# AdaLN-conditioned FFN on one Trainium2 core: another order of the first matmul's products, and of what is queued around them

## The chip, the cores and the metric

The kernel runs on one core of a Trainium2 chip. The metric is the device time of one execution in microseconds (us). It was measured three times before the change: median 1011.42 us, from 1010.62 to 1012.57.

The engines are called as in the profile: PE is TensorE, PEld its weight loads, DVE is VectorE, ACT is ScalarE, POOL is GpSimd and SP is SyncE, which issues DMAs only. All data are float32.

## The reference, cut to what matters

```python
# x: (64 batches, 64 heads, 1024 positions)
K   = 2 * real(einsum('hn,hnl->hl', Cs, exp(dtA[:, :, None] * arange(1024))))   # state-space kernel
y   = irfft(rfft(x * mask) * rfft(K)) + x * mask * D        # causal convolution along the positions
y   = y * mask                                              # "cond": 4096 tokens of width 1024
s   = y @ Wr.T                                              # router, 64 experts of rank 16
G   = zeros.at[top16(s)].set(softmax(top16 values))         # gates
h   = einsum('nd,krd->nkr', y, A)                           # first FFN matmul: 1024 -> 64*16 = 1024
out = x + 2 * einsum('nkr,kdr->nd', h * G[:, :, None], B)   # second FFN matmul: 1024 -> 1024
```

## The kernel before, in words

**Stages.** The 64 heads are eight groups of eight (`g` = 0 to 7), 512 tokens each. For every group the convolution (`conv`) makes `y`, `gates` makes the router's gates, `spread_gates` sends them through DRAM so that each arrives beside the 16 rows that it multiplies (`gx`), and `first` computes the first FFN matmul, multiplies it by the gates into the tile `hg`, and stores `hg` to DRAM. When all groups are done, `second` runs the second FFN matmul, 28 blocks of seven products, from about 668 us to the end. The groups overlap: while the convolution of group g+1 is written down, generators hand out the products of group g piece by piece (`ahead(products, n)`).

**The first matmul** is done by a Strassen-Winograd scheme in `seven`: seven products of half-size factors in place of eight, for each of two halves of the rows (`j` = 0 and 2). One product is 16 matmuls of 128x256. In groups 1 to 7 (`LOW_FROM`) the products 7 and 4 are themselves split in seven (`low`): seven small products of 8 matmuls of 128x128 each, computed for j = 0 and 2 at once and handed out in two parts. Here they are called 7a (its products 1, 6, 7, 2) and 7b (5, 4, 3), likewise 4a and 4b. Between the products DVE combines the results:

- c11 = product 1, to which product 2 is added later in the same PSUM bank; ACT copies the bank to `p1` in between (line 783, shown as `h_p`).
- `u2 = p1 - product 6` (line 793), `u3 = product 7 + u2`, shown as `h_u`.
- c12 = product 5, to which product 3 is added later in the same bank. In between DVE reads the bank to make `c22 = -u3 - c12` (line 829, which calls the helper on line 504; `h_p`), so product 3 waits for c22.
- `u2 = c12 + u2` (line 1193).

So the order of one half is, in groups 1 to 7, 1, 6, 7a, 2, 7b, 5, 3, 4a for j = 0 and 1, 4b, 6, 2, 5, 3 for j = 2.

**Gates.** `finish` allots `hg` and makes the gated quarters: b22, b12 and b21 by POOL (line 1177), b11 by DVE out of the PSUM bank (line 1184). All four are made after product 3 (b21 of j = 0 after 4b). `sums` then makes three sums on DVE (t1 = b11 - b12, b12 = b22 - b12, t2 = b22 + t1) and `last_sum` a fourth, b21 - t2, written over b11. They are run one or two pieces into the next half (`sum_factors`). POOL issues the stores to DRAM (line 1180): b11 and b22 together, b21, then b12, t1, t2, then the fourth sum. There is one buffer of `hg`: the next half's first gate waits until the last store of the one before has landed. The buffers `u2`, `u3` and `p` (for p1 and c22) are two each, and four PSUM banks (`ps_f`) hold all products.

**Order of the queues.** A planner orders each engine's instructions at build time, by the order in which they are written down and by when it takes each to be ready. The trace shows its order, which can differ from the written one. `keep_in_program_order` puts an instruction behind the one written just before it on its engine, `issue_after` behind a named one. On the chip every engine runs its queue in order, so an instruction that waits holds all behind it.

**Left factors.** For the split products 7 and 4, `left_factors` makes sums of weights by DMAs that accumulate, issued by POOL (line 690): twelve of them during group 0, six of which wait for an earlier one to land, and two more in group 1. The first of them to be needed is in product 7a of group 1, at 153.8 us.

Of the kernel before, what the change touches and what calls it, by code (L numbers as in the profile page):

```python
# [107 lines left out]
def body(ctx: ExitStack, tc, x, xo, lens, par, dvec, dgrp, at, bm, wt, cst, out):  # L108
# [601 lines left out]
    def low(n, rights, name, early, late):  # L710
# [22 lines left out]
        q6 = product(6)  # L733
        tt(v2, v2, q6[:, :, :H2], ALU.subtract)
        early(v2)
        q7 = product(7)
        tt(v3, q7[:, :, :H2], v2, ALU.add)
        product(2, c11)
        late((0, 0), c11[:, :, :H2], None, None)
        yield  # L740
        c12 = product(5, more=True)
        late((1, 1), c12[:, :, :H2], v3, v2)
# [6 lines left out]
    def seven(fac, rf, name, finish, second_early, lows):  # L749
# [26 lines left out]
            else:  # L776
                stt(o, v, -1.0, ALU.mult, bank, ALU.subtract)

        u3_of, fourth_of, open_ = {}, [], []
        for j in (0, 2):  # L780
            c11 = product(j, 1, more=True)
            p1 = new(j, "p", 1)
            marks["p1"] = nc.scalar.copy(p1, c11)
            yield j
            for step_ in open_:
                yield j
            early_ = second_early and not j
            if early_:
                product(j, 2, c11)
                yield j  # L790
            p6 = product(j, 6)
            u2 = new(j, "u2")
            marks["u"] = V.tensor_tensor(out=u2, in0=p1, in1=p6, op=ALU.subtract)
            if j in u3_of:
                u3 = u3_of[j]
                tt(u3, u3, u2, ALU.add)
            yield j
            steps_ = iter(())
            if lows and not j:
                u3 = new(j, "u3")  # L800
                other = u3_of[2] = new(2, "u3")

                def early(v, o=u3, u2=u2):
                    tt(o[:, :, hi_], u2[:, :, hi_], v, ALU.add)

                def late(place, bank, v, _, o=u3, u2=u2, other=other):
                    if place[0]:
                        other_half(place, bank, v, other[:, :, (lo_, hi_)[place[1]]])
                    elif place[1]:
                        marks["u"] = V.tensor_tensor(out=o[:, :, hi_], in0=o[:, :, hi_], in1=bank, op=ALU.add)  # L810
                    else:
                        tt(o[:, :, lo_], bank, u2[:, :, lo_], ALU.add)

                steps_ = low(7, low_rights(rf[6], f"{name}_r7"), name, early, late)
                next(steps_)
                yield j
            if not early_:
                product(j, 2, c11)
                yield j
            for _ in steps_:  # L820
                yield j
            if not lows:
                p7 = product(j, 7)
                u3 = new(j, "u3")
                marks["u"] = V.tensor_tensor(out=u3, in0=p7, in1=u2, op=ALU.add)
                yield j
            c12 = product(j, 5, more=True)
            c22 = new(j, "p", 5)
            stt(c22, u3, -1.0, ALU.mult, c12, ALU.subtract)
            if lows and j:  # L830
                for half, v in zip((lo_, hi_), fourth_of):
                    tt(u3[:, :, half], v, u3[:, :, half], ALU.subtract)
            yield j
            if not lows:
                p4 = product(j, 4)
                tt(u3, p4, u3, ALU.subtract)
                yield j
            elif not j:
                rights = low_rights(rf[3], f"{name}_r4")
            product(j, 3, c12)  # L840
            done = finish(j, c11, u2, c12, c22)
            if not lows or j:
                done(u3)
                yield j
                continue
            yield j
            fourth_of[:] = rights[6], rights[0]

            def early(v, o=u3):
                tt(o[:, :, hi_], o[:, :, hi_], v, ALU.subtract)  # L850

            def late(place, bank, v, room, o=u3):
                if place[0]:
                    other_half(place, bank, v, room)
                else:
                    half = (lo_, hi_)[place[1]]
                    tt(o[:, :, half], bank, o[:, :, half], ALU.subtract)

            def rest(steps_, done, u3):
                for _ in steps_:  # L860
                    done(u3)
                    yield

            steps_ = low(4, rights, name, early, late)
            next(steps_)
            open_ = rest(steps_, done, u3)
            yield j


    begun = {}  # L870
# [291 lines left out]
    def first(g, y, spread):  # L1162
# [4 lines left out]
        if g:  # L1167
            rf[:] = right_factors(v, f"ty{g}_")

        def finish(j, c11, u2, c12, c22):  # L1170
            hg = hp.tile([P, 6, 2, HT], F32, tag="hg", name=f"hg_{g}_{j}")

            def gate(m, s):
                return spread[m, j][:, :, s * HT : (s + 1) * HT]

            def gt_(o, a, b, op):
                G.tensor_tensor(out=o, in0=a, in1=b, op=op)  # L1177

            def store(a, b, slot):
                nc.gpsimd.dma_start(hg_dram[g, :, slot : slot + b - a, j : j + 2, :], hg[:, a:b])  # L1180

            b11, b22, b21, b12, t1, t2 = (hg[:, n] for n in range(6))
            def first_quarter():
                i = V.tensor_tensor(out=b11, in0=c11, in1=gate(0, 0), op=ALU.mult)
                if late_gates:
                    tc.keep_in_program_order(i)


            late_gates = g in (0, NG - 1)
            if not late_gates:  # L1190
                first_quarter()
            gt_(b22, c22, gate(1, 1), ALU.mult)
            marks["u"] = V.tensor_tensor(out=u2, in0=c12, in1=u2, op=ALU.add)
            gt_(b12, u2, gate(0, 1), ALU.mult)
            if late_gates:
                first_quarter()
            store(0, 2, 0)

            def sums():
                tt(t1, b11, b12, ALU.subtract)  # L1200
                tt(b12, b22, b12, ALU.subtract)
                tt(t2, b22, t1, ALU.add)
                store(3, 6, 3)

            def last_sum():
                tt(b11, b21, t2, ALU.subtract)
                store(0, 1, 6)

            def done(u3):
                gt_(b21, u3, gate(1, 0), ALU.mult)  # L1210
                store(2, 3, 2)
                unsummed.extend((sums, last_sum))

            return done

        last = None
        for j in seven(wa, rf, f"h{g}", finish, g == 0, g >= LOW_FROM):
            n = 0 if j != last else n + 1
            last = j
            if n in (1, 3 if j and g >= LOW_FROM else 2):  # L1220
                sum_factors(1)
            yield
            if n == 1 and len(rf) == 2:
# [260 lines left out]
    def ahead(it, n):  # L1484
        for _ in range(n):
            next(it, None)
# [17 lines left out]
    for g in range(NG):  # L1504
# [16 lines left out]
            products, done = counted(first(g, y, spread)), [0]  # L1521
        if g + 1 == NG:
            break
        if g == 0:
            made_left = [left_factors(n) for n in (7, 4)]
            for steps_ in made_left:
                ahead(steps_, 3)
        ahead(products, (1, 3)[g] if g < 2 else 2)
        spread_gates(g, ex, spread)
        if g == 0:  # L1530
            tables1, n = steps_of(1), 0
            while True:
# [138 lines left out]
```

## Time and profile before

| | |
|---|---|
| median of the timed runs | 1011.42 us |
| the profiled execution | 1011.2 us, of which its span is 1009.4 and 1.8 lie around it |
| busy: PE, DVE, POOL, ACT | 944.7, 778.2, 372.8, 169.6 us |
| granted TensorE clock, mean | 0.98 |
| first matmul, a product of 16 matmuls | 3.45 us start to start, of 8 small ones 0.89 us |
| `second`, 668 us to the end | PE busy 337.3 of 341.4 us |

The page has a line of engine totals, a strip of 40 slices, the chain of work that ended last, and groups of instructions by line. In a group "x16 | 38.9, 2432" is the count, the busy time in us and the mean of one in ns. The list of waits has, for each pair, the time in us, the number of waits and the longest. In a timeline the first number is the start in us, the second the duration, and a bracket at the end is the idle time just before, with what ended it. In a table of windows the columns are the window, its length, busy time (and instructions) of PE, PEld, DVE, ACT and POOL, the granted clock, the DMA share and GB/s.

### The profile page before, as it was taken

The numbers are of one execution on the slowest core, as the hardware profiler recorded it, in microseconds if no ns is written. First come the engines' busy times: TensorE is split into PE (matmuls) and PEld (weight loads), VectorE is DVE, ScalarE is ACT, GpSimd is POOL, SyncE is SP. The second block draws the span as 40 slices with busy tenths as digits, with TensorE's granted clock in tenths as the row PEclk, the third lists the DMA queues.
The fourth block names the chain that finished last, engine by engine and source line by source line (L and its number), as shares of the span: only waits on it lengthen the run. The fifth ranks groups of instructions, "written<-read, shape, count | busy, mean of one in ns | idle before, by whom it ended". The sixth has DMA issues, their size and how long they took to land.

```text
span 1009.4 us, 15219 instructions
## 1 busy us (share of the span) xinstructions
PE 944.7 (94%) x5720; PEld 759.4 (75%) x5720; DVE 778.2 (77%) x1872; ACT 169.6 (17%) x328; POOL 372.8 (37%) x330
## 2 busy tenths in 40 slices
PE   7997899998998998998998998989999999999998
PEld 2674658677667767857856877878888888888887
DVE  8984889698796796797688459879975785686674
ACT  5351122421311321231130000000000000000000
POOL 0234212132124105115106113236664774554565
PEclk9999899998999998999999999999999999999999
DMA  7769146225433434245235045384475368267432
GB/s 271 203 141 198 57 123 169 99 79 172 137 94 127 149 87 157 84 144 166 85 94 172 33 171 210 104 303 156 155 238 193 104 210 281 84 213 254 128 124 105
DMA packets 74959, 153.21 MB, mean 152 GB/s; under 512 B 10790, under 2 KB 22790, under 8 KB 74886
## 3 DMA queue, kind: packets, MB, share of 16 engines
q1 hardware_dynamic: 52546, 99.65, 30.7%
q0 software_dynamic: 19520, 50.89, 16.4%
q10 hardware_dynamic: 2820, 1.70, 0.6%
q8 instruction: 45, 0.74, 0.3%
q14 instruction: 28, 0.23, 0.1%
HBM read 100.13 MB, written 47.33 MB: 146 GB/s over the span
## 4 chain that ended last, share of the span: by engine, by line
PE 56%; DVE 24%; POOL 5%; issue 2%; DMA 2%; ACT 1%; DVEq 0%; POOLq 0%
PE s L1424 33%; PE h L760 10%; PE h L721 6%; DVE s L927 5%; POOL hg L1177 3%; DVE hg L493 2%; PE pc L992 2%; PE pc L969 2%; PE pu L883 1%; DVE s_more L927 1%; DVE h_u L493 1%; POOL gx L1148 1%; DMA gt_dram<-gt 1%; PE psh L1088 1%; DVE y L1003 1%
## 5 line engine op out<-in xcount | busy, mean ns | idle before, releaser
L760 PE MATMUL h<-y,waa 128*128 128x256 f32 x512 | 119.9, 385 | 0.0
L927 DVE SCALAR_TENSOR_TENSOR s<-s,turn 128x64 f32<-128x64 f32 (+1 forms) x432 | 116.5, 314 | 2.0 <-ACT s L888 1.3
L760 PE MATMUL h<-ty,was 128*128 128x256 f32 x512 | 117.7, 380 | 0.0
L760 PEld LDWEIGHTS h<-y,waa 128*128 128x128 f32 x512 | 97.9, 195 | 13.9 <-issue 0.7
L760 PEld LDWEIGHTS h<-ty,was 128*128 128x128 f32 x512 | 95.5, 190 | 14.8 <-issue 2.7
L1177 POOL TENSOR_TENSOR hg<-h_p,gx 128x512 f32<-128x512 f32 x16 | 38.9, 2432 | 174.3 <-DVE h_p L504 170.5
L1177 POOL TENSOR_TENSOR hg<-h_u,gx 128x512 f32<-128x512 f32 x32 | 45.4, 1419 | 124.3 <-DVE h_u L493 96.1
L760 PE MATMUL h<-y,was 128*128 128x256 f32 x288 | 68.4, 391 | 8.0 <-DVE h_p L504 8.0
L1180 POOL DMA_DIRECT2D hg_dram<-hg x64 | 43.6, 681 | 87.3 <-DVE hg L493 31.3
L760 PEld LDWEIGHTS h<-y,was 128*128 128x128 f32 x288 | 54.4, 194 | 19.4 <-DVE h_p L504 11.1
L1438 ACT COPY p<-s 128x512 f32<-128x512 f32 x28 | 16.4, 586 | 307.9 <-PE s L1424 307.9
L493 DVE TENSOR_TENSOR hg<-hg 128x512 f32<-128x512 f32 x64 | 42.6, 682 | 33.0 <-POOL hg L1177 27.7
L1283 POOL TENSOR_TENSOR o<-o,acc_a 128x512 f32<-128x512 f32 x32 | 47.6, 1508 | 41.3 <-ACT acc_a L1301 10.8
L883 PE MATMUL pu<-x,bt 128*64 128x448 f32 x256 | 53.4, 549 | 3.1 <-DVE y L1003 3.1
L1003 DVE TENSOR_TENSOR y<-pc,mask 128x512 f32<-128x512 f32 x64 | 40.6, 682 | 16.5 <-PE pc L992 16.5
L1148 POOL DMA_DIRECT2D gx<-gt_dram x56 | 34.3, 649 | 50.0 <-DMA gt_dram<-gt 47.2
L1283 POOL TENSOR_TENSOR o<-o,b_room 128x512 f32<-128x512 f32 x32 | 49.6, 1572 | 8.6 <-DVE b_room L493 8.6
L493 DVE TENSOR_TENSOR o<-o,s 128x512 f32<-128x512 f32 x50 | 34.0, 680 | 21.9 <-PE s L1424 16.8
L992 PE MATMUL pc<-s,w 64*64 64x192 f32 (+1 forms) x768 | 42.4, 368 | 7.9 <-DVE s L927 7.9
L1283 POOL TENSOR_TENSOR o<-o,u 128x512 f32<-128x512 f32 x36 | 45.8, 1295 | 10.0 <-DVE u L493 9.7
L721 PE MATMUL h<-h_r,low 128*128 128x128 f32 x224 | 30.4, 279 | 16.3 <-DVE h_r L493 16.3
L883 PEld LDWEIGHTS pu<-x,bt 128*64 128x64 f32 x256 | 17.4, 137 | 35.7 <-issue 16.7
(313 smaller groups left out, 1941.8 us busy)
## 6 DMA issues: line engine op xcount, KB each, us to landing
x<-in_x SPq DMA_DIRECT2D x32, 512.0 KB
o<-in_xo SPq DMA_DIRECT2D x64, 256.0 KB
out<-o SPq DMA_DIRECT2D x63, 256.0 KB
gx<-gt_dram POOLq DMA_DIRECT2D x56, 256.0 KB, 4.5
qy<-hg_dram SPq DMA_DIRECT2D x28, 512.0 KB
r<-hg_dram SPq DMA_DIRECT2D x26, 512.0 KB
hg_dram<-hg POOLq DMA_DIRECT2D x16, 768.0 KB, 5.2
hg_dram<-hg POOLq DMA_DIRECT2D x16, 512.0 KB, 4.7
```

The lines of the kernel that those rows point to most:

```text
L493: V.tensor_tensor(out=o, in0=a, in1=b, op=o_)
L721: nc.tensor.matmul(bank[:, ii, :H2], lhsT=LOW[n][i - 1][:, k, ii * P : (ii + 1) * P], rhs=rights[i - 1][:, k, :], start=(first and ii == 0 ...
L760: nc.tensor.matmul(bank[:, ii, :], lhsT=fac[n - 1][:, k, (j + ii) * P : (j + ii + 1) * P], rhs=rf[n - 1][:, k, :], start=(first and ii == ...
L883: nc.tensor.matmul(pu[hh * NS : (hh + 1) * NS, :], lhsT=bt[:, i, (1 - c) * P + hh * NS : (1 - c) * P + (hh + 1) * NS], rhs=xt[:, hh, : NCH ...
L927: return V.scalar_tensor_tensor(out=o, in0=a, scalar=scalar, in1=b, op0=op0, op1=op1)
L992: m = nc.tensor.matmul(pcs[hh][half_of(e, late), into], lhsT=w[o : o + NS, c, i, seg : seg + HP], rhs=s[o : o + NS, c, of].rearrange("p k ...
L1003: marks["y"] = V.tensor_tensor(out=y[:, :, i // 2, 2 * (i % 2) + hh, :], in0=pcs[hh].rearrange("p (k b) -> p k b", b=NB), in1=mask, op=ALU ...
L1148: i = queue.dma_start(gx[:, ii, :], gt_dram[g, c * n : (c + 1) * n, :].unsqueeze(1).to_broadcast([n, RANK, TOK]),)
L1177: G.tensor_tensor(out=o, in0=a, in1=b, op=op)
L1180: nc.gpsimd.dma_start(hg_dram[g, :, slot : slot + b - a, j : j + 2, :], hg[:, a:b])
L1283: tc.keep_in_program_order(G.tensor_tensor(out=o, in0=a, in1=b, op=op_))
L1424: nc.tensor.matmul(bank[:, ii, :], lhsT=left_[i - 1][:, k, ii * P : (ii + 1) * P], rhs=right_[i - 1][:, k, :], start=(first and ii == rows ...
```

## The change

In groups 1 to 7 the order of the products becomes 1, 5, 6, 7a, 3, 7b, 2, 4a for j = 0 and 1, 5, 4b, 6, 3, 2 for j = 2: again fourteen pieces, handed out at the same places of the convolution. Product 5's bank is copied to `p5` by ACT, and c22 is made later out of `p5`, in place. Products 1 and 5 thus both hold their banks until products 2 and 3 are added. The four gated quarters are made as their inputs come: b12 after product 3, b22 after u3 is whole, b11 after product 2, b21 after 4b (for j = 2, b12, b22 and b21 after product 3, b11 after product 2). `sums` and `last_sum` are run two pieces apart, after the third and the fifth piece of a half's successor instead of the second and the third (fourth for j = 2); `last_sum` writes over t1 instead of b11. Within a split product, product 2 comes ahead of product 7. Group 0 keeps its order of products, but makes b21 ahead of b12. In the main loop the left factors' DMAs are written behind the gates' DMAs of group 0 instead of ahead of them.

```diff
@@ low
         early(v2)
+        product(2, c11)
+        late((0, 0), c11[:, :, :H2], None, None)
         q7 = product(7)
         tt(v3, q7[:, :, :H2], v2, ALU.add)
-        product(2, c11)
-        late((0, 0), c11[:, :, :H2], None, None)
         yield
@@ seven, groups 1 to 7 (group 0 keeps the old order in a branch of its own)
+        def first_two(j):
+            c11 = product(j, 1, more=True)
+            p1 = new(j, "p", 1)
+            marks["p1"] = nc.scalar.copy(p1, c11)
+            yield c11, p1
+            c12 = product(j, 5, more=True)
+            p5 = new(j, "p", 5)
+            nc.scalar.copy(p5, c12)
+            yield c12, p5
...
+        def into_22(p5, u3):
+            marks["u"] = V.scalar_tensor_tensor(
+                out=p5, in0=u3, scalar=-1.0, in1=p5, op0=ALU.mult, op1=ALU.subtract)
+            return p5
...
+        seventh = low(7, low_rights(rf[6], f"{name}_r7"), name, early, late)
+        next(seventh)
+        yield 0
+        product(0, 3, c12)
+        last_12(c12, u2)
+        yield 0
+        next(seventh)
+        last_22(into_22(p5, u3))
+        yield 0
+        product(0, 2, c11)
+        last_11(c11)
+        rights = low_rights(rf[3], f"{name}_r4")
+        yield 0
...
+        fourth = low(4, rights, name, early, late)
+        next(fourth)
+        yield 0
+        steps = first_two(2)
...
+        next(fourth)
+        last_21(u3)
+        yield 2
+        u2 = sixth(2, p1)
+        tt(other, other, u2, ALU.add)
+        yield 2
+        last_12, last_22, last_11, last_21 = finish(2)
+        product(2, 3, c12)
+        last_12(c12, u2)
+        last_22(into_22(p5, other))
+        for half, v in zip(halves, (rights[6], rights[0])):
+            tt(other[:, :, half], v, other[:, :, half], ALU.subtract)
+        last_21(other)
+        yield 2
+        product(2, 2, c11)
+        last_11(c11)
+        yield 2
@@ finish
+            def last_12(c12, u2):
+                marks["u"] = V.tensor_tensor(out=u2, in0=c12, in1=u2, op=ALU.add)
+                gt_(b12, u2, gate(0, 1), ALU.mult)
+            def last_22(c22):
+                gt_(b22, c22, gate(1, 1), ALU.mult)
+            def last_21(u3):
+                gt_(b21, u3, gate(1, 0), ALU.mult)
+                store(2, 3, 2)
+                unsummed.append(last_sum)
+            def last_11(c11):
                 i = V.tensor_tensor(out=b11, in0=c11, in1=gate(0, 0), op=ALU.mult)
                 if late_gates:
                     tc.keep_in_program_order(i)
+                store(0, 2, 0)
+                unsummed.insert(0, sums)
...
             def last_sum():
-                tt(b11, b21, t2, ALU.subtract)
-                store(0, 1, 6)
+                tt(t1, b21, t2, ALU.subtract)
+                store(4, 5, 6)
@@ first
-            if n in (1, 3 if j and g >= LOW_FROM else 2):
+            if n in ((1, 2) if g < LOW_FROM else ((2, 4) if j == 0 else (2, 4))):
                 sum_factors(1)
@@ the main loop
+        ahead(products, (1, 3)[g] if g < 2 else 2)
+        spread_gates(g, ex, spread)
         if g == 0:
             made_left = [left_factors(n) for n in (7, 4)]
             for steps_ in made_left:
                 ahead(steps_, 3)
-        ahead(products, (1, 3)[g] if g < 2 else 2)
-        spread_gates(g, ex, spread)
```

## The prediction

> **What bounds the kernel now.** I read the engine totals first, then the waits of PE and DVE, then the timelines around the longest of them, then a table by stage.
>
> ```profile
> PE 944.7 (94%) x5720; PEld 759.4 (75%) x5720; DVE 778.2 (77%) x1872; ACT 169.6 (17%) x328; POOL 372.8 (37%) x330
> ```
>
> PE's products fill the span, so only time in which PE stands still, or runs at a lower clock, is to be had: 1009.4 - 944.7 = 64.7 us, and the low clock. The second matmul has next to none of it (341.4 us, 337.3 busy) and the change does not touch it. The waits of PE, and under them the two of DVE that are not for PE, say whom it waits for in the rest:
>
> ```profile
> PE h L721 <- DVE h_r L493: 16.3, 6, 3.1
> PE h L760 <- DVE h_p L504: 8.0, 7, 2.9
> PE pc L992 <- DVE s L927: 7.9, 2, 7.5
> PE h L721 <- DVE ty L504: 4.6, 4, 1.3
> PE h L721 <- DVE h_u L793: 4.6, 6, 1.0
> ```
>
> ```profile
> DVE hg L493 <- POOL hg L1177: 27.7, 10, 4.5
> DVE hg L1184 <- DMA gx<-gt_dram: 15.2, 1, 15.2
> ```
>
> PE waits for DVE, and DVE itself waits for POOL's gates and for one late transfer. The same stretch comes once a group; here it is in group 5, from the timeline:
>
> ```profile
> 460.70 4.60 POOL L1177 TENSOR_TENSOR hg<-h_p,gx 128x512 f32<-128x512 f32 x1
> ...
> 466.62 1.28 POOL L1177 TENSOR_TENSOR hg<-h_u,gx 128x512 f32<-128x512 f32 x1
> ...
> 469.46 1.28 POOL L1177 TENSOR_TENSOR hg<-h_u,gx 128x512 f32<-128x512 f32 x1
> ...
> 470.77 0.69 DVE L493 TENSOR_TENSOR hg<-hg 128x512 f32<-128x512 f32 x1 [4.39 <-POOL hg L1177]
> ...
> 473.48 1.13 PE L721 MATMUL h<-h_r,low 128*128 128x128 f32 x8 [3.12 <-DVE h_r L493]
> ...
> 475.52 3.56 PE L721 MATMUL h<-y,was 128*128 128x128 f32 x16 [0.91 <-DVE h_u L793]
> ```
>
> DVE reaches `sums` of the previous half and stands 4.39 us for the third gate, b12, which ends at 470.74. The factors of product 7a (`h_r`) and u2 lie behind it in DVE's queue, so PE stands 3.12 and 0.91 us. In group 0 the late transfer does the same (timelines of POOL, DVE and PE):
>
> ```profile
> 80.28 0.85 POOL L690 DMA_DIRECT2D low<-low  x1 [3.79 <-DMA low<-low]
> 80.87 3.90 POOL L1148 DMA_DIRECT2D gx<-gt_dram  x6
> ...
> 89.04 0.69 DVE L1184 TENSOR_TENSOR hg<-h,gx 128x512 f32<-128x512 f32 x1 [15.22 <-DMA gx<-gt_dram]
> ...
> 100.25 0.92 PE L992 MATMUL pc<-s,w 64*64 64x192 f32 x8 [7.49 <-DVE s L927]
> ```
>
> ACT sends the gates to DRAM at 64.87, but POOL is busy with the left factors until 80.87, so b11's factor comes at 89.0. DVE then does the recurrences (L927) 15 us late, and PE runs dry. Each such dry spell is followed by a low clock (the granted clock is the last number but two):
>
> ```profile
> 84.00:137.00 53.00, 40.09 (x295) 29.80 (x296) 39.31 (x110) 6.19 (x15) 17.33 (x20) 0.84 0.61 155
> 380.00:460.00 80.00, 73.13 (x516) 56.98 (x514) 64.50 (x187) 19.31 (x35) 20.68 (x22) 0.96 0.39 124
> 460.00:538.00 78.00, 72.34 (x517) 56.60 (x517) 61.07 (x176) 13.42 (x25) 21.21 (x23) 0.98 0.37 118
> ```
>
> **Group 0: the transfers in their new order.** The gates' data can go when they are in DRAM: 64.87 + 3.1 (group 5: sent at 455.80, first `gx` issued at 458.88) = 68.0. An issue takes 0.62, so the first pair is out by 69.3 and lands 4.5 later by the median of its line (3.5 to 11.2): 73.7, from 72.7 to 80.4. DVE arrives at b11 at 73.8. It waits 0 to 6.7 instead of 15.2; I take 2, so DVE runs 13 us ahead. Its unbroken work from 89.65 to the end of c22 at 120.35 (30.7 us) then ends near 107. PE reaches that product at 92.76 + 3.03 + 3 x 3.45 = 106.1. So of PE's idle time between 84 and 137 (7.49, 0.39, 2.87 and 2.16 for the convolution's results, 12.9 in all) about 11 goes; 1.0 of the last stays, as in later groups (1.03), and 0.6 before c22. The low clock costs 53 x 0.16 = 8.5 us of half-filled time, 5.5 of it while PE works; I take 4 back. Gain 15. The ceiling is 12.9 + 5.5 = 18. What moves: twelve DMA issues of the left factors, 31 us of POOL's queue from 50.05 to 81.1, now start near 73 and would end at 104 or later. First use is at 153.8, so that hides. But the gates of group 0 (92.3 to 97.2) share that queue. If all stood behind it, they would end near 109, and `sums`, at 102.02 now, would be 7 us late: the low end is -7. I expect them between the DMAs: these leave POOL idle 3.0 to 3.8 us six times, and the planner does mix the two (in group 1 two left-factor DMAs, at 123.91 and 124.86, run ahead of a gate, at 126.56, that is written before them).
>
> **Groups 2 to 6: the sums two products on.** Between product 3 of j = 2 and `sums` lie now two products (1 and 6, 6.9 us); after the change four (2, 1, 5, 6; 13.8 us). POOL needs 3 x 1.3 us for the three gates, or 4.6 + 2 x 1.3 with the slow one, from about 1 us after product 3: done by 5 to 9 us, so DVE finds them ready. The stalls in front of 7a are gone: 2.77 + 4 x 3.12 for `h_r` and 1.04 + 0.91 + 0.64 + 0.91 + 0.91 for u2, 19.7 us. The low clock of the stages of groups 2 to 6 (82 x 0.04, 80 x 0.02, 80 x 0.04, 78 x 0.02, 70 x 0.02) is 11.1 us, about 10 while PE works; all of it lies just behind 7a, so 10 goes with the stall. The row that decides this is a dry spell of 3.12 us, which sufficed for a low clock.
>
> The Trainium skill (TensorE: Matmul & The Clock Gate, Part 1) says that the clock halves after an idle window of about 3.4 us. By that, spells of 3.12 would cost nothing and these 10 us would not come back; the trace shows the low clock behind each, and I go by it.
>
> **ACT's copy of the fifth product.** Fourteen copies more at 0.586 us (line 783) are 8.2 us on an engine that is busy 17%; they hide beside product 6, and product 3 comes more than 7 us later. PE no longer waits for c22: 0.89, 0.94, 0.93, 0.94, 0.93 and 0.50 in groups 1 to 6, 5.1 us. c22 stays one DVE instruction of 0.68. A copy needs a free `p`, so it waits for POOL's b22 of the half before: ready 10.5 us after that half's product 3, the gate done by 9. If POOL is 1 us late or more, ACT holds the copy inside 7a too, but 4 us of cover lie there. I take nothing.
>
> GPSIMD Engine Reference (of the skill) warns that its data path is shared with DVE instructions of two SBUF inputs, and c22 becomes one. The slow gate, 4.60 us beside DVE's wide sums, agrees, and in price it would be some 0.7 us of POOL per half.
>
> **Two banks held through 7a and 4b.** Products 1 and 5 hold two of the four banks, so small product 6 needs the bank that u2 frees. After the small product before it (0.89) u2 needs a pick-up of about 0.25 (product ends seen in the timeline) and 0.68: 0.04 us late if DVE is free, more by what runs there (0.2 to 1.7). I take 0.6 there, 0.3 for small product 7 and 0.3 in 4b: 1.2 x 7 groups = 8 us, between 0 and 20. The waits for `ty` (4.6 us, 4b behind the router's DVE work) get a product of cover more; I take nothing for that, at most 4.6.
>
> **The sum.** 15 + 19.7 + 10 + 5.1 - 8 = 41.8. From the profiled execution's 1011.2 (0.2 below the median) that is 969.4; I say 969. Group 7 is filled by DVE (54.28 of 60 us), so I expect no more there.
>
> **Rivals.** (1) DVE's stall comes back in another place, or the planner runs `sums` where it likes: `sums` of j = 0 ran at 506.60, ahead of 4b (521.7), though written behind it. Then 7a and its clock stay: 969 + 19.7 + 10 = 999, or 991 if the banks then cost nothing. For it: DVE's order is the planner's, and POOL's 4.6 us was not foreseen. Against: twice the distance. (2) Slower: `last_sum` now overwrites t1, which is still being read by the store of 768 KB that `sums` sets off; before it overwrote b11, whose store left 8 us earlier (465.85 to 473.93). Price: issue 0.7 and landing 5.2 after the sums' 2.0 us, 7.9, against two products of cover (6.9) and about 1 us of other DVE work: nothing at the median, but at the longest landing (8.8) 3.6 us in each of 14 halves, in front of u2, plus a wait for the single `hg` buffer, since the next half's gates are written just ahead of `last_sum`: one more store of 256 KB, 0.7 + 3.9 on POOL and, through b11, on DVE. If the second alone reaches PE, 14 x 4.6 = 64 us: 969 + 64 = 1033. It makes the kernel slower from 41.8 / 14 = 3.0 us a half. Against: DVE waited for these stores twice, 5.2 us in all. (3) The move has no effect, because the left factors' transfers still go first: 969 + 15 = 984.
>
> **Numbers.** Forecast with its bank costs 0.60 (955 to 984), rival 1 0.18, rival 3 0.05, rival 2 0.17. Best case 1011.2 - 18 - 34.8 - 4.6 = 954. From 954 to 1005 leaves out about 0.2. A time within 0.2% (2 us, what a measurement here can tell) of before needs rival 2 at just its turning point: 0.03. Faster 0.80, slower 0.17.
>
> **What would show it.** Right: `gx` of group 0 issued near 68, DVE's wait in front of b11 under 7 us, no 7.5 us gap of PE near 93; no wait of DVE `hg` for POOL above 1 us; PE's waits for `h_r` under 3 us in all, `h_p` near none, waits for u2 in L721 of 0.3 to 1 us, more often than now; granted clock 1.00 in groups 2 to 6. Wrong: DVE `hg` or L1184 waiting for a store (`hg_dram`) for several us a half, or PE's waits for `h_u` above 20 us.

## The result: slower, and the profile after

The changed kernel takes 1043.33 us (median of 4 runs, 1040.55 to 1044.71) against 1011.33 before: a ratio of 1.0312 (95% interval 1.0287 to 1.0336). The forecast was 969. The profiled execution took 1044.08 us with a span of 1042.3; lines behind the diff stand 40 later than before (u2 of product 6: L829; u2 of `last_12`: L1226; POOL's gates: L1217).

The engine totals, with share of the span and instruction count:

```profile
PE 951.0 (91%) x5720; PEld 765.2 (73%) x5720; DVE 800.2 (77%) x1872; ACT 178.6 (17%) x342; POOL 357.2 (34%) x330
```

Of the 32.9 us by which the span grew, PE stands still for 26.6 more (1042.3 - 951.0 = 91.3 against 64.7) and is busy 6.3 longer at the same instruction count, which goes with the lower granted clock (mean 0.961 against 0.980). Neither half of the forecast's gain came; both moved the other way.

The waits of PE, then those of DVE (total us, times, longest):

```profile
PE h L721 <- DVE h_u L829: 37.5, 7, 7.9
PE h L721 <- DVE h_u L504: 10.0, 4, 3.5
PE pu L923 <- DVE y L1043: 8.4, 1, 8.4
PE s L1464 <- DVE acc_a L493: 7.9, 1, 7.9
PE h L721 <- ACT y L732: 7.1, 1, 7.1
...
PE h L760 <- DVE h_p L504: 2.8, 1, 2.8
```

```profile
DVE hg L493 <- DMA hg_dram<-hg: 41.5, 8, 9.9
...
DVE hg L493 <- POOL hg L1217: 3.0, 2, 1.6
```

What was to go did go: no row names `h_r`, `h_p` fell from 8.0 to 2.8, and DVE's waits for POOL's gates from 27.7 to 3.0. In their place PE waits 37.5 us for u2 of product 6, seven times, and DVE 41.5 us for stores to `hg_dram`. (The wait called "in front of 7a" stands, before and after, just behind 7a's first small product.) These are the two signs that the forecast named as showing it wrong. Group 5's timeline (POOL, then DVE, then PE) shows how they hang together:

```profile
478.20 2.13 POOL L1217 TENSOR_TENSOR hg<-h_u,gx 128x512 f32<-128x512 f32 x1
...
485.51 1.81 POOL L1188 DMA_DIRECT2D gx<-gt_dram  x3
487.28 0.80 POOL L1220 DMA_DIRECT2D hg_dram<-hg  x1
...
482.04 1.28 DVE L967 SCALAR_TENSOR_TENSOR s<-s,turn 128x64 f32<-128x64 f32 x1
483.25 1.28 DVE L493 TENSOR_TENSOR hg<-hg 128x512 f32<-128x512 f32 x2
...
489.69 0.27 DVE L967 SCALAR_TENSOR_TENSOR s_more<-s_more,turn 128x64 f32<-128x64 f32 x1
495.25 0.69 DVE L493 TENSOR_TENSOR hg<-hg 128x512 f32<-128x512 f32 x1 [5.29 <-DMA hg_dram<-hg]
495.86 0.68 DVE L829 TENSOR_TENSOR h_u<-h_p,h 128x512 f32<-128x512 f32 x1
...
487.65 1.05 PE L721 MATMUL h<-y,was 128*128 128x128 f32 x8
496.60 1.65 PE L721 MATMUL h<-h_r,low 128*128 128x128 f32 x6 [7.89 <-DVE h_u L829]
```

The sums end near 484.5. Their store of 768 KB goes out only at 487.28, behind three `gx` issues on POOL, and lands near 495.2. DVE runs recurrences (L967) until 489.9 and then stands 5.29 us with the fourth sum, which must not overwrite t1 before the store has read it. u2 could run when product 6 ends at about 487.7, but stands behind both, although it is written two pieces ahead of the fourth sum. The next small product needs the bank that u2 frees, so PE stands 7.89 us.

Group 0, by the timelines of POOL, DVE and PE:

```profile
67.50 4.85 POOL L1188 DMA_DIRECT2D gx<-gt_dram  x8 [17.53 <-DMA gt_dram<-gt]
...
73.57 0.68 DVE L1238 TENSOR_TENSOR hg<-h,gx 128x512 f32<-128x512 f32 x1
...
109.02 5.41 PE L760 MATMUL h<-y,was 128*128 128x256 f32 x16 [2.83 <-DVE h_p L504]
...
118.80 1.78 POOL L690 DMA_DIRECT2D waa<-waa  x1
119.83 1.55 POOL L1220 DMA_DIRECT2D hg_dram<-hg  x1
...
130.53 0.69 DVE L493 TENSOR_TENSOR hg<-hg 128x512 f32<-128x512 f32 x1 [9.94 <-DMA hg_dram<-hg]
...
131.88 2.51 PE L923 MATMUL pu<-x,bt 128*64 128x448 f32 x6 [8.36 <-DVE y L1043]
```

The product behind c22, before the change:

```profile
120.41 5.34 PE L760 MATMUL h<-y,was 128*128 128x256 f32 x16 [2.87 <-DVE h_p L504]
```

The transfers start where the forecast put them (67.50; b11 at 73.57 without a wait), and that product starts at 109.02 instead of 120.41. Then the store of the sums goes out behind the last of the left factors' transfers, the fourth sum waits 9.94 us, and PE stands 8.36. The same happens at the other end of the kernel: the last half's fourth sum runs inside the second matmul, which the forecast took as untouched, waits 9.61 us for its store, and PE stands 7.9 us for DVE's `acc_a` behind it.

The granted clock by stretches (the last number but two) fell just where it was to rise. These are group 2 before, then groups 2 and 5 after (group 5 before, 0.98, stands in the prediction):

```profile
218.00:300.00 82.00, 74.52 (x521) 58.29 (x522) 70.07 (x208) 19.32 (x35) 24.03 (x26) 0.96 0.42 124
...
222.00:304.00 82.00, 66.28 (x470) 50.66 (x469) 64.36 (x187) 24.18 (x42) 13.49 (x18) 0.88 0.43 123
470.00:556.00 86.00, 75.38 (x520) 59.29 (x519) 64.50 (x177) 14.57 (x27) 19.63 (x23) 0.92 0.33 106
```

### The profile page after: what moved, and what is told of

It is laid out like the page before. It is cut to its first block, busy times and chain, and to the rows that moved or that the text cites. A ratio compares the mean times of both kernels' runs of the same rounds, so it can differ in the third digit from the quotient of the medians.

```text
span 1042.3 us, 15267 instructions
## 1 busy us (share of the span) xinstructions
PE 951.0 (91%) x5720; PEld 765.2 (73%) x5720; DVE 800.2 (77%) x1872; ACT 178.6 (17%) x342; POOL 357.2 (34%) x330
## 4 chain that ended last, share of the span: by engine, by line
PE 51%; DVE 22%; DMA 7%; issue 5%; POOL 3%; ACT 2%; DVEq 0%; POOLq 0%; ACTq 0%
PE s L1464 30%; PE h L760 7%; PE h L721 6%; DMA hg_dram<-hg 6%; DVE s L967 4%; PE pc L1032 2%; POOL hg L1217 2%; DVE ty L493 2%; PE pu L923 1%; DVE hg L493 1%; DVE y L1043 1%; PE pc L1009 1%; DVE h_u L493 1%; PE psh L1128 1%; DMA rmag<-rows_of 1%
## 5 line engine op out<-in xcount | busy, mean ns | idle before, releaser
L967 DVE SCALAR_TENSOR_TENSOR s<-s,turn 128x64 f32<-128x64 f32 (+1 forms) x432 | 127.6, 341 | 2.6 <-ACT s L928 2.2
L1217 POOL TENSOR_TENSOR hg<-h_u,gx 128x512 f32<-128x512 f32 x32 | 48.7, 1538 | 216.6 <-DVE den L498 95.3
L493 DVE TENSOR_TENSOR hg<-hg 128x512 f32<-128x512 f32 x64 | 45.2, 722 | 45.2 <-DMA hg_dram<-hg 41.5
L760 PE MATMUL h<-y,was 128*128 128x256 f32 x288 | 70.9, 392 | 2.8 <-DVE h_p L504 2.8
L721 PE MATMUL h<-h_r,low 128*128 128x128 f32 x224 | 35.5, 308 | 37.5 <-DVE h_u L829 37.5
L721 PEld LDWEIGHTS h<-h_r,low 128*128 128x128 f32 x224 | 31.9, 216 | 41.8 <-DVE h_u L829 39.4
L1323 POOL TENSOR_TENSOR o<-o,acc_a 128x512 f32<-128x512 f32 x32 | 47.6, 1506 | 41.4 <-DMA qy<-hg_dram 10.8
L493 DVE TENSOR_TENSOR o<-o,s 128x512 f32<-128x512 f32 x50 | 34.0, 681 | 23.0 <-PE s L1464 17.9
L967 DVE SCALAR_TENSOR_TENSOR s_more<-s_more,turn 128x128 f32<-128x128 f32 x144 | 47.1, 327 | 0.0
```

What stands on the lines that cost most here:

```text
L493: V.tensor_tensor(out=o, in0=a, in1=b, op=o_)
L721: nc.tensor.matmul(bank[:, ii, :H2], lhsT=LOW[n][i - 1][:, k, ii * P : (ii + 1) * P], rhs=rights[i - 1][:, k, :], start=(first and ii == 0 ...
L760: nc.tensor.matmul(bank[:, ii, :], lhsT=fac[n - 1][:, k, (j + ii) * P : (j + ii + 1) * P], rhs=rf[n - 1][:, k, :], start=(first and ii == ...
L967: return V.scalar_tensor_tensor(out=o, in0=a, scalar=scalar, in1=b, op0=op0, op1=op1)
L1323: tc.keep_in_program_order(G.tensor_tensor(out=o, in0=a, in1=b, op=op_))
```

## The experiments

Two theories stood at the start. The theory of the store: the fourth sum's wait is the loss. The theory of the banks: u2 is wanted at once in 7a, and anything ahead of it on DVE is the loss. Each time below is a median; each ratio is to the kernel before in the same runs, whose medians lay between 1010.44 and 1013.73.

### Parts of the change, undone or done alone

**The fourth sum back over b11**, in the changed kernel:

```diff
-                tt(t1, b21, t2, ALU.subtract)
-                store(4, 5, 6)
+                tt(b11, b21, t2, ALU.subtract)
+                store(0, 1, 6)
```

> The changed kernel with one line put back: the fourth sum is written over b11 again instead of t1. Theory of the store (the fourth sum waits for the store that the three sums before it have just set off, and u2 and the evictions queue behind it on DVE): DVE's waits for stores of hg fall from 41.5 us to under 8, and with them PE's gaps that are their image, 20 us in front of product 7a in groups 2 to 6, 8.4 in group 0 and 7.9 at the start of the second matmul; about 36 us less: 1000 to 1012 us. Theory of the banks (products 1 and 5 hold two of four banks, so small product 6 waits for u2 whatever DVE does just before): the waits for stores go too, but PE's wait for u2 at L829 stays above 25 us of its 37.5, and the time stays above 1022.

1032.33 us, ratio 1.0208 (1.0182 to 1.0233); the time and PE's wait are as the theory of the banks had them. The line is worth 11 us of the 32. The waits of DVE and of PE:

```profile
DVE hg L493 <- DMA hg_dram<-hg: 19.1, 7, 7.5
...
PE h L721 <- DVE h_u L829: 31.9, 7, 6.8
```

DVE's wait more than halves, PE's in front of 7a hardly moves: b11 has a store of its own to wait for, and recurrences fill the rest.

**The same line alone in the kernel before** (that diff read backwards):

> The kernel before with the one line changed: the fourth sum is written over t1, nothing else. Theory of the store: the fourth sum follows the three within 1 to 3 us there, and the store takes 0.7 us to issue and 5.2 to land, so DVE waits 3 to 6 us in most of the sixteen halves and PE behind it: 1030 to 1060 us. Theory of the banks: order and banks are those of before, so 1008 to 1015 us.

1024.77 us, ratio 1.0139 (1.0124 to 1.0154), between the two expectations: the line costs 14 us in the old order too.

**The left factors' transfers behind the first gates, alone in the kernel before:**

```diff
+        ahead(products, (1, 3)[g] if g < 2 else 2)
+        spread_gates(g, ex, spread)
         if g == 0:
             made_left = [left_factors(n) for n in (7, 4)]
 ...
-        ahead(products, (1, 3)[g] if g < 2 else 2)
-        spread_gates(g, ex, spread)
```

> The kernel before with only the left factors' transfers written behind the gates of group 0. As forecast: DVE's 15.2 us wait in front of b11 in group 0 goes, PE's 7.5 us gap near 100 us too, and the kernel gains 10 to 18 us: 993 to 1001. Rival: the later left factors delay the gates and stores of group 0 on POOL and in the DMA queue, DVE waits there instead, and the time stays within 5 us of 1011.

1003.58 us, ratio 0.9933 (0.9916 to 0.9950): a gain of 7, between the two expectations. DVE's timeline says where the rest stayed:

```profile
120.30 2.02 DVE L493 TENSOR_TENSOR hg<-hg 128x512 f32<-128x512 f32 x3 [8.19 <-POOL hg L1177]
```

The sums wait 8.19 us for the last gate, which stands on POOL among the transfers, and PE 9.41 us later on for `y`.

**That part undone in the changed kernel** (the same lines read backwards):

> The changed kernel with the left factors' transfers written ahead of the gates again. If that move alone gains 10 to 15 us, as forecast, this is slower than the changed kernel's 1043: 1052 to 1060. Rival: in the changed kernel the last left factors' transfers run just ahead of the stores that the fourth sum of group 0 waits 9.9 us for, and moving them back takes that wait away and gives the gain of the move back elsewhere: 1040 to 1048.

1057.57 us, ratio 1.0479 (1.0437 to 1.0521): 14 us slower, so inside the change the move gained about what was forecast.

### What stands ahead of u2

Four runs of the changed kernel with DVE's queue reordered in front of 7a. **Recurrences of pairs 2 and 3 behind u2:**

```diff
-            marks["u"] = V.tensor_tensor(out=u2, in0=p1, in1=p6, op=ALU.subtract)
+            marks["u"] = marks["six"] = V.tensor_tensor(out=u2, in0=p1, in1=p6, op=ALU.subtract)
 ...
-        recur(2, 3)
+        with tc.issue_after(marks["six" if g > 1 else "u"].ins):
+            recur(2, 3)
```

> After the change, with the recurrences of pairs 2 and 3 queued on DVE behind u2 of product 6 of j = 2 (groups 2 to 6) instead of wherever the planner puts them. In group 5 u2 stood ready at 487.65 and ran at 495.86: until 489.9 behind recurrences, then behind the fourth sum, which waits for the 768 KB store that lands at 495.2. Theory of the store: the landing alone sets the time, taking the recurrences away leaves the DVE waits for the store larger by what they covered (41.5 to about 55 us) and PE's wait in front of 7a near 37 us: 1040 to 1045. Theory of the queue (whatever stands ahead of u2 while small product 6 lacks a bank costs PE its length): the recurrences cost about 3.5 us a half in groups 2 to 6, so PE's wait falls to 20 us or less: 1022 to 1030.

1040.20 us, ratio 1.0265 (1.0230 to 1.0300), as the theory of the store had it. (In the trace the recurrences follow u2 of j = 0, at 494.64 in group 5, and not of j = 2, as the expectation says.) DVE's wait for stores grew from 41.5 to 66.0 us and PE's for u2 fell only to 31.2: the recurrences had run inside the wait and cost little while it lasted.

**The fourth sum behind the u2 written last** (that of product 3, L1226):

```diff
-                tt(t1, b21, t2, ALU.subtract)
+                with tc.issue_after(marks["u"].ins):
+                    tt(t1, b21, t2, ALU.subtract)
```

> After the change, with the fourth sum (still into t1, still behind the 768 KB store) queued on DVE behind the u2 sums of the small products and of the next half, so that its wait stands ahead of nothing that PE needs at once. Theory of the store: PE's wait in front of 7a falls from 37.5 us to the part that the recurrences make (about 16 us): 1018 to 1025, clearly better than the fourth sum over b11 (1032). Theory of the queue: the place is taken by the recurrences and by the gates written behind it, PE's wait in front of 7a stays at 25 to 32 us as with the sum over b11: 1028 to 1036.

1023.70 us (1016.24 to 1027.10), ratio 1.0096 (1.0066 to 1.0126). It gains 20, more than the 11 of writing over b11; what remains in front of 7a (26.8 us in the profiled run) is, in group 5, recurrences.

**Both:**

> After the change with both: recurrences of pairs 2 and 3 and the fourth sum queued behind u2. If what stands ahead of u2 is the whole loss in front of 7a, PE's waits for h_u fall from 37.5 to below 8 us, the clock of groups 2 to 6 rises to about 0.99, and the time is 1043 - 30 - 10 = 1000 to 1006, below the kernel before. If the two held banks cost by themselves (u2 must be picked up and run within one small product), 1 to 2 us stay in each of 7 groups and the time is 1010 to 1018.

1017.15 us, ratio 1.0060 (1.0031 to 1.0088). The waits of PE:

```profile
PE h L721 <- DVE h_u L504: 23.6, 5, 6.1
...
PE h L721 <- DVE h_u L829: 7.3, 3, 3.7
```

The wait in front of 7a falls below 8 us, as the first expectation had it, but the time is that of the second. 7b waits 23.6 us: its third small product is added to the bank of its first, which DVE has to read before (L504), and that reading now stands behind the recurrences and the convolution's evictions.

**ACT frees the bank of product 6:**

```diff
-            marks["u"] = V.tensor_tensor(out=u2, in0=p1, in1=p6, op=ALU.subtract)
+            nc.scalar.copy(u2, p6)
+            marks["u"] = V.tensor_tensor(out=u2, in0=p1, in1=u2, op=ALU.subtract)
```

> After the change, with product 6 copied out of its bank by ACT (0.59 us) and u2 formed from the copy, so that the bank is free without DVE, whatever stands in DVE's queue. Theory of the banks: small product 6 starts about 0.8 us after the bank is copied, PE's wait in front of small product 6 goes (37.5 us in all), part of it comes back where the next small products need DVE's early and late evictions: 1015 to 1028. Theory of the store (and of DVE's queue as a whole): DVE stands until the landing anyway and every eviction of 7a is behind it, so the wait only moves one or two small products on, to lines of 7a: 1036 to 1043.

1039.63 us, ratio 1.0258 (1.0215 to 1.0302). PE's timeline in group 5:

```profile
491.56 1.11 PE L721 MATMUL h<-h_r,low 128*128 128x128 f32 x8
492.51 1.06 PE L721 MATMUL h<-y,was 128*128 128x128 f32 x8
498.93 2.08 PE L721 MATMUL h<-y,was 128*128 128x128 f32 x8 [5.37 <-DVE y L493]
```

The bank is free and the small product runs at once; PE stops two small products on, for the next thing that DVE owes. PE's waits for DVE in 7a fell from 37.5 to 27.0 us, but in group 2 a wait for ACT grew from 7.1 to 13.1. The theory of the banks falls in its narrow form: in group 5 the bank only decides at which instruction PE meets DVE's queue.

**Product 6 before product 5**, so that u2 has a whole product of cover, first alone, then with the fourth sum behind u2:

```diff
         c11, p1 = next(steps)
         yield 0
-        c12, p5 = next(steps)
-        yield 0
         u2 = sixth(0, p1)
         yield 0
+        c12, p5 = next(steps)
+        yield 0
```

> After the change, with product 6 of j = 0 before product 5 instead of behind it, so that u2 has a whole product (3.45 us) in which to free its bank; the small products, the sums and the fourth sum stay as they are. Theory of the banks (u2 is late because only one small product lies between it and the product that needs its bank): PE's wait in front of 7a (37.5 us, 7 times) falls by up to 3.45 each, to 13 to 20 us, and the time is 1015 to 1025. Theory of the store (DVE stands until the store lands, at 495.2 in group 5, and nothing that DVE must do comes earlier): the wait keeps its size, only one product of cover later or earlier: 1036 to 1044.

1032.35 us, ratio 1.0220 (1.0193 to 1.0246), between the two expectations: u2's wait falls from 37.5 to 8.3 us, and 16.0 come back in front of the last small products of 7a (`y`, L493), in group 5 because DVE still stands for the store (5.11 us).

> After the change, with product 6 of j = 0 before product 5, and the fourth sum queued behind u2. With the fourth sum behind u2 alone the time was 1023.7, and 3.7 to 6.6 us stayed in front of each 7a (26.8 in all), put down to recurrences ahead of u2. If that rest is the price of the held bank, a product of cover takes nearly all of it: PE's waits for u2 below 8 us, time 998 to 1008. If the wait only follows DVE's queue, it moves on to 7b and the time stays at 1015 to 1024.

1013.28 us (1004.97 to 1015.88), ratio 1.0006 (0.9982 to 1.0031), between the two expectations: level with before, not better. u2 still came about 2.5 us late, behind recurrences that the planner put there.

**The fourth sum on POOL**, with product 6 first:

```diff
-                tt(t1, b21, t2, ALU.subtract)
+                gt_(t1, b21, t2, ALU.subtract)
```

> After the change, product 6 before product 5 (alone 1032.4), and the fourth sum done by POOL instead of DVE, so that POOL, not DVE, stands for the store of 768 KB. Theory of the store: DVE's waits for hg_dram (30.7 us in that run) fall below 5, and the time falls as far as with the fourth sum queued behind u2 (1013) or further, 1005 to 1016. Theory of DVE's load: 5 to 10 us are got at most (1022 to 1030), because recurrences and evictions fill the place; and POOL's wait holds up the next half's gates, since all of them share hg.

1007.93 us, ratio 0.9951 (0.9931 to 0.9972). DVE's list of waits names no store any more. The wait itself is still there, on POOL (62.2 us, 12 times); that it left DVE's queue brought 24 us against the run with product 6 first alone, and 19 of these came in the run before, with the sum still on DVE.

### Why the gains did not come

With store and bank out of the way the new order was only level. The next runs ask whether the 19.7 us of stalls and the low clock behind them could be had at all. **The sums one or two steps later, in the old order:**

```diff
-            if n in (1, 3 if j and g >= LOW_FROM else 2):
+            if n in ((1, 2) if g < LOW_FROM else (2, 4)):
```

> The kernel before, with its order of products, and only the point moved at which the sums of a finished half are written: in groups 2 to 6 the second and fourth step of each half (before: the first, and the second or third). This is the term of 19.7 us (stalls in front of 7a behind DVE's wait for POOL's gates) and 10 us (low clock) tried alone. If the term was right and the new order ate it: PE's waits for h_r fall from 16.3 to below 4 us, DVE's hg waits for POOL from 27.7 to below 10, time 982 to 992. If the stall is DVE's load and only takes another name (y, ty or u2): 1003 to 1012.

1016.40 us, ratio 1.0065 (1.0043 to 1.0087): outside both expectations. DVE and PE in group 5:

```profile
468.96 0.69 DVE L493 TENSOR_TENSOR hg<-hg 128x512 f32<-128x512 f32 x1 [2.58 <-POOL hg L1177]
...
470.24 0.42 DVE L493 TENSOR_TENSOR h_r<-y,h_r 128x256 f32<-128x256 f32 x1
...
472.64 0.68 DVE L793 TENSOR_TENSOR h_u<-h_p,h 128x512 f32<-128x512 f32 x1
...
470.13 1.13 PE L721 MATMUL h<-h_r,low 128*128 128x128 f32 x8 [1.59 <-DVE h_r L493]
473.38 1.94 PE L721 MATMUL h<-y,was 128*128 128x128 f32 x9 [2.12 <-DVE h_u L793]
```

Written later, the sums still stand ahead of the last `h_r` and of u2 on DVE. 3.12 + 0.91 became 1.59 + 2.12, and the low clock came as before.

**The same with the left factors' move** (both edits above):

> The kernel before, with its order of products, with the left factors' transfers behind the first gates and the sums' point moved as in the run beside it. The transfers alone gave 7 us (1003.6). If both terms are independent the time is that of the sums' run less 7: 975 to 985 if the sums' term holds, 996 to 1005 if it doesn't.

1010.15 us, ratio 0.9979 (0.9952 to 1.0005): above both expectations, but the two parts add up within the noise (-7 and +4 to +7).

**The sums queued behind u2 of product 6, in the old order**, alone and with the left factors' move (the condition takes in groups 1 to 7):

```diff
-                sum_factors(1)
+                with (tc.issue_after(marks["u"].ins) if j == 0 and g >= LOW_FROM else nullcontext()): sum_factors(1)
```

> The kernel before with one edit: the sums of groups 2 to 6 behind u2 of product 6 of j = 0. With the transfers too it was 992.4; the transfers alone gave 7 us. If the two add up: 998 to 1001. If DVE's place in front of 7a alone is worth the forecast's 19.7 and 10 us: 982 to 990, and the transfers then give little besides. If it is worth nothing without them: 1008 to 1012.

1003.15 us, ratio 0.9890 (0.9847 to 0.9934): a gain of 11, between the 998 to 1001 of two terms that add up and the 1008 to 1012 of none.

> The kernel before with two edits: the left factors' transfers behind the first gates (alone 1003.6), and in groups 2 to 6 the sums of the half before queued on DVE behind u2 of product 6 of j = 0, not ahead of the factors of 7a. Theory of the queue (what counts is which instruction stands in front on DVE; POOL's slow gate may be waited for once PE has its factors): PE's waits for h_r (16.3 us) go, the low clock behind them too, 1003.6 - 16 - 8 = 975 to 985. Theory of DVE's load: the same work stands later in front of 7a's evictions or of 7b; waits for h_u, y and ty take the place: 998 to 1010.

992.39 us (985.28 to 996.52), ratio 0.9793 (0.9735 to 0.9852), between the two expectations. DVE and PE in group 5:

```profile
450.02 1.98 DVE L493 TENSOR_TENSOR h_r<-y,h_r 128x256 f32<-128x256 f32 x1
...
453.82 0.28 DVE L927 SCALAR_TENSOR_TENSOR s_more<-s_more,turn 128x64 f32<-128x64 f32 x1
454.01 0.68 DVE L793 TENSOR_TENSOR h_u<-h_p,h 128x512 f32<-128x512 f32 x1
454.61 2.01 DVE L493 TENSOR_TENSOR hg<-hg 128x512 f32<-128x512 f32 x3
...
454.75 3.62 PE L721 MATMUL h<-y,was 128*128 128x128 f32 x16 [2.51 <-DVE h_u L793]
```

Here the sums no longer wait for POOL and stand ahead of nothing that PE lacks; PE's wait for `h_r` is gone in groups 2 to 6. What is left is 2.51 us for u2, behind recurrences that run from 451.92.

**The recurrences behind u2 as well**, on top of that run:

```diff
-            marks["u"] = V.tensor_tensor(out=u2, in0=p1, in1=p6, op=ALU.subtract)
+            marks["u"] = marks["six" if j == 0 else "six2"] = V.tensor_tensor(out=u2, in0=p1, in1=p6, op=ALU.subtract)
 ...
-        recur(2, 3)
+        with tc.issue_after(marks["six" if g > 1 else "u"].ins):
+            recur(2, 3)
```

> The kernel before with the left factors' transfers behind the first gates, the sums of groups 2 to 6 behind u2 of product 6 of j = 0 (together 992.4), and the recurrences of pairs 2 and 3 behind the same u2. In that run u2 came 2.5 us late in five groups, behind 2 us of recurrences. Theory of the queue: these 5 x 2.5 = 12.5 us go, and part of the low clock: 978 to 986. Theory of DVE's load: the recurrences come back in front of 7b or of the convolution's results (y), as when the same was done in the new order: 988 to 996.

973.05 us (971.98 to 978.77), ratio 0.9608 (0.9574 to 0.9642): below both expectations and the fastest version, 70 us below the changed kernel. Its totals, group 5 on DVE and PE, and the windows of groups 4 and 5:

```profile
PE 932.9 (96%) x5720; PEld 750.0 (77%) x5720; DVE 794.4 (82%) x1872; ACT 169.5 (17%) x328; POOL 361.3 (37%) x330
```

```profile
439.27 0.68 DVE L793 TENSOR_TENSOR h_u<-h_p,h 128x512 f32<-128x512 f32 x1
439.86 0.68 DVE L493 TENSOR_TENSOR hg<-hg 128x512 f32<-128x512 f32 x1
440.46 0.34 DVE L927 SCALAR_TENSOR_TENSOR s<-s,turn 128x128 f32<-128x128 f32 x1
...
440.00 2.05 PE L721 MATMUL h<-y,was 128*128 128x128 f32 x16
```

```profile
360.00:437.00 77.00, 72.76 (x527) 56.59 (x526) 68.98 (x190) 19.93 (x37) 20.52 (x24) 1.00 0.43 134
437.00:512.00 75.00, 72.32 (x526) 56.33 (x525) 64.37 (x177) 12.60 (x23) 20.41 (x24) 1.00 0.39 124
```

u2 runs 1.2 us after product 6 ends, no wait stands behind it, and the clock stays at 1.00. Idle time is 972.1 - 932.9 = 39.2 us against 64.7 before; PE is busy 11.8 us less.

### The new order with the same treatment

**Product 6 first, sums, fourth sum and recurrences all behind u2**; the recurrences and the fourth sum as above, the sums so:

```diff
-                sum_factors(1)
+                with (tc.issue_after(marks["six"].ins) if j == 0 and n == 2 and g >= LOW_FROM else nullcontext()): sum_factors(1)
```

> After the change, product 6 before product 5, and in groups 2 to 6 the sums, the fourth sum and the recurrences of pairs 2 and 3 all queued behind u2 of product 6. Nothing movable then stands ahead of the bank's release, and u2 has a product of cover. Theory of the queue: PE's waits for u2 (L829) fall below 2 us, 7b's rise by a part, time 995 to 1006. Theory of DVE's load: 7b waits 5 to 7 us in each of five groups as it did when u2 was put ahead of the recurrences only, and the time is 1010 to 1020.

1010.45 us (1000.06 to 1013.80), ratio 0.9974 (0.9944 to 1.0004). u2's waits fell as the theory of the queue says, but the time is that of DVE's load. PE's waits name 7b:

```profile
PE h L721 <- DVE h_u L504: 14.3, 4, 4.2
```

Here, unlike in the old order, the reading of its first bank stands on DVE behind the convolution's evictions, and the fourth sum is still on DVE, which waits 17.1 us for its stores.

**Product 6 first, fourth sum on POOL, sums behind u2** (this last edit with the one on POOL):

> After the change, product 6 before product 5, fourth sum on POOL (these two together 1007.9), and the sums of groups 2 to 6 queued behind u2 of product 6. If only the queue was at fault, the new order now does what the old one did with the same treatment: 990 to 998. If the new order has a cost of its own (7b behind the convolution's evictions, 2 us in each of four groups; ACT's wait of 6 us in group 2, with a low clock behind it), it stays at 1000 to 1008.

995.29 us, ratio 0.9816 (0.9791 to 0.9841). This is about what the old order reached with transfers and sums alone (992.39). No version of the new order tried here was faster than the old order with like treatment. Two things keep that from being the last word: the new order with the fourth sum on POOL and both sums and recurrences behind u2 was not run, and every run of it has a stall in group 2 that the old order lacks (6.9 us here; see the next section).

## Why the prediction was wrong, step by step

- **What bounds the kernel** was read rightly: DVE's queue in front of 7a, and the low clock behind the stall. The fastest version gains about 40 us (ratio 0.9608) by those two and the left factors' move. That it is near the 41.8 of the sum is no support for the sum's terms: the means are other than the change's.
- **Sums two products on** (-19.7) is the step that failed first. That DVE would find the gates ready was right (27.7 to 3.0 us). That PE's stall in front of 7a would go with them was not: `h_r` no longer waits, but u2 does, 37.5 us. The step counted products between sums and gates; what counts is which instructions the planner leaves ahead of `h_r` and u2 on DVE. Written later in the old order, without a place in the queue, the sums made it 4 to 7 us slower (1016.40); queued behind u2, with no other edit, they brought 11 us (1003.15), and the recurrences' place another 19 (992.39 to 973.05).
- **The low clock** (-10) follows the stall, as the step said; since the stall grew, it cost more. The step read 3.12 us as enough for a low clock, but in groups 3 to 6 that stall is followed 1.1 us of work later by one of 0.64 to 0.91, so the row does not show it for 3.12 alone.
- **Two banks held** (+8, 0 to 20) was mis-sized. It allowed 0.2 to 1.7 us for "what runs there" on DVE, from the rows of before. The planner runs recurrences there (484.45 to 489.9 in group 5, 2.2 us of them past product 6), and the fourth sum with its wait: 37.5 us in front of 7a and 10.0 in front of 7b. The two run side by side: moving the recurrences alone took 6.3 us off PE's wait for u2, moving the fourth sum alone 10.7, moving both 30.2 (37.5 to 7.3).
- **Rival 2** named the right mechanism at the wrong price. It had the store land 5.9 us behind the sums, against two products of cover. In group 5 it was issued 2.8 us after the sums' end, behind POOL's `gx` issues, and landed 10.8 after it; and the wait stood in front of u2, wanted 3.2 us after the sums. The two products of cover were not there, because the planner ran the fourth sum ahead of u2. Nor is it the whole loss: undoing it gave 11 us, taking it from in front of u2 gave 20.
- **Group 0** (-15, -7 to 18): the start times and the b11 wait came as worked out, and the product behind c22 came 11 us earlier, where DVE was to be 13 ahead. Inside the change the move is worth about 14 (1057.57 without it). Alone the move gave 7, for the reason that the step gave as its low end: the second half's gates and the store stand among the transfers on POOL.
- **ACT's copy** (-5.1): c22's waits went in groups 1 to 6, as forecast; group 0's stayed (2.83 us where 0.6 was forecast).
- **Not seen at all**: in group 2, ACT stood 12.76 us for a transfer of the next convolution's tables (`rmag`, issued at 232.6 instead of 213.8), and PE 7.1 us for ACT's `y`. It is in every run of the new order, at 4.2 to 13.1 us; what sends that transfer late was not tried and is open.

## What to carry to other kernels

Where a planner fills an engine's queue, moving an instruction in the program moves only when it may run. Ask which instruction has to come first on that engine, and queue everything movable behind it; that was worth some 30 us here, while no run showed a gain from the new order of products. When several waits stand side by side ahead of the same instruction, take them away together before judging any of them, and look where the wait turns up next: here 14 of the 30 us that left 7a came back in 7b.

Before overwriting a buffer, follow its store through the issuing queue to its landing, and price the wait by what stands behind the waiting instruction, not by the wait itself.

## What the runs showed of the hardware

- **A gate on POOL and a DVE instruction beside it slow each other, now one, now the other.** Before, the slow gate took 4.60 us beside DVE's wide sums, where the others take 1.28. After, at 478 to 484.5, it is DVE: a recurrence that takes 0.27 us elsewhere took 1.28 and ended with the gate beside it (481.53 to 483.24). The Trainium skill (GPSIMD Engine Reference, Specifications) says that the two share their SBUF interfaces and contend when a DVE instruction has two SBUF inputs. The sums and the recurrence have two, and in these rows now one side paid, now the other.
- **The clock falls without a long gap.** With the sums later in the old order (1016.40), waits of 1.2 to 1.6 and 2.1 to 2.2 us with 1.1 us of work between them were followed by a low clock in all five groups from 2 to 6, as before the change 2.8 to 3.1 and then 0.6 to 1.0 were. A lone wait of 2.5 to 2.9 was so in two groups of five in one version (992.39) and three in another (1003.15), one of 1.83 in none (973.05). In the clock records of these traces the low stretches last 3.41, 6.83, 10.24 or 13.65 us, all multiples of 3.41. That agrees with the free-running window of 3.4 us in the skill's TensorE: Matmul & The Clock Gate (Part 1); the rule there that the clock halves after at least one idle window of about 3.4 us does not fit these runs, in which no single wait of those groups is that long.
